# Attention and clustering block: group norms and cluster counts rearranged, filler work dealt out anew

## The chip, the cores and the metric

The kernel runs on one core of a Trainium2 chip, in 32-bit floating point. The metric is the device time of one execution in microseconds, as a median of several runs. A profile of one further execution gives the trace.

## The reference, cut to what matters

Four images `x` of 256 channels and 64 x 64 pixels go through two layers. Layer 0 is full self-attention over the 4096 pixels. Layer 1 is a clustering block, an MLP and a pointwise product:

```python
x = gamma * (v @ softmax(q^T k)^T) + x                      # layer 0
xn = group_norm(x)                                          # over all channels and pixels of an image
feat, val = conv1x1(xn, f_w), conv1x1(xn, v_w)              # 4 heads of 24 channels
# each image and head in 2 x 2 folds of 32 x 32 pixels; in each, 4 centres m (means of 16 x 16 cells)
sim = sigmoid(beta + alpha * cosine(centres, points))       # [m, n]
mask = one_hot(argmax over m); sim = sim * mask
agg = (sum_n sim[m, n] * val[n] + val_centre[m]) / (mask.sum(-1) + 1.0)
out[n] = sum_m sim[m, n] * agg[m]
y = x + ls1 * conv1x1(out, proj_w)
y = y + ls2 * mlp(group_norm(y))                            # 256 -> 1024 -> gelu -> 256
z = relu(bn(conv1x1(relu(bn(y * dw_w)), pw_w)))
```

The group norm has one group: a mean and a variance over the whole image. `mask.sum(-1)` counts the points that a centre has won.

## The kernel before

The images are worked on one after the other. For each there is an attention stage, a clustering stage (`cluster`) and an MLP stage (`mlp`). The order of every engine's instructions is the order in which the program writes them (`manual_schedule`); nothing is reordered by a planner.

**Fillers.** Where the clustering stage has short dependent steps, TensorE gets independent work to do. It is a list of small jobs, `todo`, and `fill(n)` takes the next n of them. In images 0 to 2 the list holds the projections of the next image's attention, 35 jobs: 32 halves of `v` (L316; after each second one ACT copies a finished pair out of PSUM, L324), two halves of `k` (L293, `kp`) and one of `q` (L335, `qp`). In image 3 there is no next image. There the list holds the MLP of the last 512 pixels of image 2 (`late_block`, L1073 `hlp`, L1090 `mol`, L1116 `pwl`). `fill(N)` empties the list.

**Group norm.** `group_norm` is called as `gn1` at the head of the clustering stage, and as `gn2` at the head of the MLP. The per-partition statistics are merged by L245 into `mv`. Two products with one column each (L247, L248, `gnm`) give a partition's distance from the mean, and the mean. A filler follows. On VectorE L251 copies both to `dv`, L252 adds the squared distance to the variance, L255 negates the mean. A third product (L257, `gnv`) averages the variance; `rsqrt` is L173 (add eps, VectorE), L174 (square root, ACT), a callback `meanwhile`, and L176 (reciprocal, VectorE). L265 and L266 make the factors `ga` and `gb`. In `gn1` the callback is `pooling`: it first sums the last block of pixels into its cells (`rest`, L523), then makes the pooled means (L703, L704), which L723 normalizes and `pcen` (L728) projects. In `gn2` a small ACT instruction makes ACT load the Gelu table after the last filler of the group norm (`table`, L239).

**Clustering.** The normalized image goes through the `fv` products (L866) in eight blocks. For each, VectorE writes values and raw similarities (L875, L882), and `heads` squares and sums lengths (L846 on POOL, or on VectorE for the last block; L847). `similar(f)` scales one half of the similarities and applies a tanh, `affine(f)` (L821) turns that into the sigmoid, `largest(f)` (L826 to L832) makes the one-hot mask `oh`, `weights(f)` (L836) multiplies both into `sim`. `affine(0)` is done within the loop over blocks, at the eighth. `summed` (L896) is 32 small products that add to `agg`: once with the pooling matrix, once with `sim`. The counts are 8 products of a matrix of ones with slices of `oh` (L922, `cnt`). Then L931 to L933 make the divisors `rc`, `sim` is transposed (L940), the sums are copied (L930) and transposed (`aggt`, L949), L953 makes the centres' values and `gp` (L961) projects them. The `op` products (L983) bring them back to the pixels; VectorE adds them (L995) and takes the statistics for `gn2` (L976), ACT and POOL do the other half (L1007, L1008).

**MLP.** Four POOL additions prepare weight combinations (L1171, L1172, L1173, L1176). The first block of the image is normalized (L1190) and combined (L1253 to L1256, on VectorE); then `first(nb, j)` makes a quarter of the hidden layer with seven products (`hp`, `hq`, `hr`, L1373).

Each 32-bit product appears in the trace as two records; 8 `cnt` products in four images are 64 records.

Of the kernel before, what the change touches and what calls it, by code (L numbers as in the profile page):

```python
# [9 lines left out]
AF = mybir.ActivationFunctionType  # L10
ALU = mybir.AluOpType
AX = mybir.AxisListType
# [33 lines left out]
def attention_then_cluster_block(  # L46
# [190 lines left out]
    def table(f):  # L237

        nc.scalar.activation(probe, probe, f)  # L239

    def group_norm(b, which, stats, fill, meanwhile=lambda: None):

        nm = f"{which}_{b}"
        mv = small.tile([P, 2], F32, tag="mv", name=f"mv_{nm}")
        nc.vector.bn_aggr(mv, stats.rearrange("p i s -> p (i s)"))  # L245
        ps1 = ps_a.tile([P, NB], F32, tag="a0", name=f"gnm_{nm}")
        nc.tensor.matmul(ps1[:, 0:1], left, mv[:, 0:1], start=True, stop=True)  # L247
        nc.tensor.matmul(ps1[:, 1:2], avg, mv[:, 0:1], start=True, stop=True)  # L248
        fill(1 if which == "gn1" else 2)
        dv = small.tile([P, 2], F32, tag="dv", name=f"dv_{nm}")  # L250
        nc.vector.tensor_copy(dv, ps1[:, 0:2])  # L251
        nc.vector.scalar_tensor_tensor(  # L252
            mv[:, 1:2], dv[:, 0:1], dv[:, 0:1], mv[:, 1:2], ALU.mult, ALU.add
        )
        nc.vector.tensor_scalar(dv[:, 1:2], dv[:, 1:2], -1.0, None, ALU.mult)  # L255
        ps2 = ps_a.tile([P, NB], F32, tag="a1", name=f"gnv_{nm}")
        nc.tensor.matmul(ps2[:, 0:1], avg, mv[:, 1:2], start=True, stop=True)  # L257
        rstd = small.tile([P, 1], F32, tag="rstd", name=f"rstd_{nm}")
        rsqrt(rstd, ps2[:, 0:1], GN_EPS, meanwhile)
        fill(3 if which == "gn1" else 1)  # L260
        if which == "gn2":
            table(AF.Gelu_apprx_tanh)
        ga = small.tile([P, KC], F32, tag="ga", name=f"ga_{nm}")
        gb = small.tile([P, KC], F32, tag="gb", name=f"gb_{nm}")
        nc.vector.tensor_scalar(ga, par(f"{which}_w"), rstd, None, ALU.mult)  # L265
        nc.vector.scalar_tensor_tensor(gb, ga, dv[:, 1:2], par(f"{which}_b"), ALU.mult, ALU.add)  # L266
        return ga, gb
# [428 lines left out]
    def cluster(b, ys, stats, cells, rest, fill, gelu, nxt, maxima):  # L696
# [1 line left out]
        pool = small.tile([P, KC, 4, 4], F32, tag="pool", bufs=1, name=f"pool_{b}")  # L698

        def pooling():  # L700
            rest()
            rows = cells.rearrange("p k (r two) a -> p k r two a", two=2)
            nc.vector.tensor_tensor(pool, rows[:, :, :, 0], rows[:, :, :, 1], ALU.add)  # L703
            nc.vector.tensor_scalar(pool, pool, 1.0 / 256, None, ALU.mult)  # L704

        ga, gb = group_norm(b, "gn1", stats, fill, pooling)
        xns, mix = {}, own_w["mix"]

        def norm(nb):
# [100 lines left out]
        def similar(f):  # L810

            sg = sgs[f]
            rsqrt(prns[f], prns[f], L2_EPS, lambda: table(AF.Gelu_apprx_tanh))
            nc.vector.tensor_tensor(quad(sg), quad(sg), over_m(prns[f]), ALU.mult)
            nc.scalar.activation(sg, sg, AF.Tanh, scale=ab[:, 0:1], bias=ab[:, 1:2])
            if f == 0:
                gelu(0)
                table(AF.Sqrt)

        def affine(f):  # L820
            nc.vector.tensor_scalar(sgs[f], sgs[f], 0.5, 0.5, ALU.mult, ALU.add)  # L821

        def largest(f):

            sg, o, best = sgs[f], oh[:, f * 256 : (f + 1) * 256], bests[f]
            nc.vector.tensor_reduce(best, quad(sg), AX.X, ALU.max)  # L826
            nc.vector.tensor_tensor(quad(o), quad(sg), over_m(best), ALU.is_equal)
            nc.vector.tensor_tensor(
                quad(o), quad(o), rank.unsqueeze(1).to_broadcast([P, 64, 4]), ALU.mult
            )  # L830
            nc.vector.tensor_reduce(best, quad(o), AX.X, ALU.max)
            nc.vector.tensor_tensor(quad(o), quad(o), over_m(best), ALU.is_equal)  # L832

        def weights(f):
            s = sim[:, :, 2 * f : 2 * f + 2, :16].rearrange("p j q s -> p q j s")
            nc.vector.tensor_tensor(  # L836
                s, folded(sgs[f]), folded(oh[:, f * 256 : (f + 1) * 256]), ALU.mult
            )

        later = {6: lambda: similar(0), 7: lambda: affine(0)}  # L840

        def heads(nb):

# [49 lines left out]
        def summed(w, first):  # L893
            for j in range(8):
                for q in range(4):
                    nc.tensor.matmul(  # L896
                        agg_p[q * 32 : (q + 1) * 32, :ED],
                        w(j, q),
                        vf[2 * (q // 2) + j // 4][:, (j // 2) % 2, 2 * (q % 2) + j % 2, ED:],
                        start=(first and j == 0),  # L900
                        stop=(not first and j == 7),
                    )

        fill(2)
        summed(lambda j, q: pool_w[:, j], True)
        heads(NBLK - 1)
        similar(1)
        fill(2)
        gelu(1)
        fill(3)  # L910
        table(AF.Sqrt)

        largest(0)
        affine(1)
        largest(1)
        weights(0)
        weights(1)

        cnt_p = ps_a.tile([P, NB], F32, tag="a1", name=f"cnt_{b}")
        ohs = oh.rearrange("p (q j s) -> p q j s", q=4, j=8)  # L920
        for j in range(8):
            nc.tensor.matmul(  # L922
                cnt_p[:ED, :64].rearrange("p (q s) -> p q s", q=4),
                ones[:, :ED],
                ohs[:, :, j],
                start=(j == 0),
                stop=(j == 7),
            )
        summed(lambda j, q: sim[:, j, q, :], False)
        nc.scalar.copy(sums, agg_p[:, :ED])  # L930
        nc.vector.tensor_scalar(rc[:ED], cnt_p[:ED, :64], 1.0, None, ALU.add)  # L931
        nc.vector.reciprocal(rc[:ED], rc[:ED])
# [225 lines left out]
    def mlp(b, ys, stats2, fill, nxt, blocks, turned, maxima):  # L1158
# [15 lines left out]
        few = swap.tile([P, h_n + 3, P], F32, tag="mix", name=f"w2_3_{b}")  # L1174
        w3_s, (pw_bcd, pw_bac, pw_abcd) = few[:, :h_n], (few[:, h_n + i] for i in range(3))
        nc.gpsimd.tensor_tensor(w3_s, s2_s, a12_s, ALU.add)  # L1176
        ga, gb = group_norm(b, "gn2", stats2, fill)
        fill(N)
        ob = out[b].rearrange("(k p) h w -> p k (h w)", p=P)
        pairs = {}  # L1180

# [286 lines left out]
        for nb in range(blocks):  # L1468
            end = nb == blocks - 1
            for j in range(4):  # L1470
                if j > 1:
                    rest()
                pw = (lambda: last(nb - 1, True, nc.gpsimd)) if end and j == 2 else lambda: None
                hs = first(nb, j, todo, slots, pw)
                if j > 1:
                    rest()
                if j == 0:
                    if nb:
                        rectify = finish(nb - 1, acc)
                    acc = [  # L1480
                        ps_a.tile([P, NB], F32, tag=f"a{c}", name=f"mo{c}_{b}_{nb}")
                        for c in range(KC)
                    ]
                    if not end:
                        acc += [
                            ps_m.tile([P, NB], F32, tag="m", name=f"mo{c}_{b}_{nb}")
                            for c in range(2, 4)
                        ]
                    elif nxt:

                        nc.sync.dma_start(
                            out=a21_s, in_=w2.rearrange("(k p) m -> p k m", p=P)[:, :h_n, P:]
                        )
                        nxt.q_block(1, nc.sync)
                elif j == 1:
                    assert not drips and not hooks
                    if nb:
                        rectify()
                    if not end:
                        ahead = norm(nb + 1, nc.gpsimd)  # L1500
                        if nb:
                            own = factors(nc.gpsimd, pairs[nb - 1][:, 1], pairs[nb - 1][:, 0])
                        else:
                            own = left_factors()
                elif j == 2 and nb and not end:
                    pointwise(nb - 1)
                scored = nxt and (nb, j) in at
                if scored:
                    copies = []
                    nxt.score(at[nb, j], copies, maxima)  # L1510
                    copies.pop()()
                if len(acc) == KC:
                    todo = second(nb, acc, hs, j)
                    slots = (2, 1, 1, 0) if scored else (0, 1, 1, 2)
                else:
                    todo = second_by_seven(nb, acc, hs, j, own, ahead)
                    slots = (0, 2, 2, 3)
                    if scored:
                        slots = (3, 1, 2, 1)
                    elif j == 2 and nb:  # L1520
                        slots = (3, 1, 0, 3)
# [131 lines left out]
```

## Time and profile before

| what | value |
|---|---|
| median of 3 runs | 3354.04 us (3353.42 to 3360.92) |
| the profiled execution | 3351.63 us, of which the trace spans 3349.9 us |
| TensorE busy (PE) | 3302.7 us, 99% |
| VectorE busy (DVE) | 2225.7 us, 66% |
| GpSimd busy (POOL) | 1930.9 us, 58% |
| ScalarE busy (ACT) | 1683.3 us, 50% |
| mean granted clock of TensorE | 0.998 |

Starts of the clustering stage's marks in the trace, in us:

| | image 0 | image 1 | image 2 | image 3 |
|---|---|---|---|---|
| first `gnm` | 580.63 | 1410.59 | 2241.71 | 3048.42 |
| first `fv` | 589.27 | 1419.24 | 2250.36 | 3056.95 |
| `gp` | 625.40 | 1455.37 | 2286.49 | 3092.95 |
| second `gnm` | 643.57 | 1473.54 | 2304.66 | 3111.21 |
| first `hp` | 648.66 | 1480.31 | 2309.75 | 3118.18 |
| second `hp` | 653.11 | 1484.40 | 2314.20 | 3125.18 |

In the profile PE is TensorE's products, PEld its weight loads, DVE VectorE, POOL GpSimd. A group's line gives the program line, the engine, the operation, the tiles and shapes, the count, the busy time and mean duration, and the idle time before it with what ended it. The granted clock is the share of full speed at which TensorE was allowed to run.

### The profile page before, as it was taken

Reading aid. Unit: us, or ns where it says so; the run is one execution under the profiler, and the core shown is the slowest. Engines: PE = TensorE matmul, PEld = TensorE weight load, DVE = VectorE, ACT = ScalarE, POOL = GpSimd, SP = SyncE. Lnnn points to the kernel's source line nnn. Section 1 sums busy time; section 2 is a strip of 40 time slices with the busy share of each in tenths; the row PEclk is TensorE's granted clock in tenths of the full one; section 3 lists DMA queues with packets and bytes.
Section 4 is the critical chain, followed back from the end, with each engine's and each line's share of the span. In section 5 each row is a group of like instructions: output and inputs, shape, how many; then the busy total and the mean of one; then the engine's idle time right before and its main releaser. Section 6 shows DMA issues by size and latency. Waiting matters only on the chain.

```text
span 3349.9 us, 34778 instructions
## 1 busy us (share of the span) xinstructions
PE 3302.7 (99%) x12322; PEld 1807.3 (54%) x12322; DVE 2225.7 (66%) x3546; ACT 1683.3 (50%) x2253; POOL 1930.9 (58%) x1366
## 2 busy tenths in 40 slices
PE   8999999999999999999999999999999999999999
PEld 4334444788533444578844344457873344346686
DVE  5667764677666766467766676647766766765775
ACT  5545553545555554355455555435555555544444
POOL 2655666366365676646635566554644676673664
PEclk9999999999999999999999999999999999999999
DMA  2000002000000000200000000020000000010000
GB/s 72 13 13 10 15 8 87 4 13 20 27 12 13 13 13 21 73 4 20 19 24 13 10 13 13 22 71 4 20 26 13 13 13 13 10 40 1 13 20 26
DMA packets 43102, 70.99 MB, mean 21 GB/s; under 512 B 9680, under 2 KB 18480, under 8 KB 42928
## 3 DMA queue, kind: packets, MB, share of 16 engines
q1 hardware_dynamic: 37040, 60.83, 5.5%
q10 hardware_dynamic: 5632, 7.41, 0.9%
q8 instruction: 97, 1.59, 0.2%
q14 instruction: 77, 0.63, 0.1%
q0 software_dynamic: 256, 0.52, 0.1%
HBM read 43.46 MB, written 16.89 MB: 18 GB/s over the span
## 4 chain that ended last, share of the span: by engine, by line
PE 94%; DVE 4%; POOL 1%; ACT 1%; issue 0%; DMA 0%; ACTq 0%; POOLq 0%; DVEq 0%
PE av L479 54%; PE mo L1290 9%; PE sc L365 8%; PE hq L1373 5%; PE hp L1373 3%; PE hr L1373 3%; PE fv L866 3%; PE vp L316 2%; PE mo L1274 1%; DVE st L976 1%; PE hq_pw L1373 1%; PE pw L1229 1%; PE hr_pw L1373 1%; PE hp_pw L1373 1%; DVE x L995 0%; PE qp L335 0%
## 5 line engine op out<-in xcount | busy, mean ns | idle before, releaser
L479 PE MATMUL av<-s,v 128*128 128x512 f32 x4096 | 1819.2, 598 | 0.6 <-ACT s L469 0.6
L474 POOL TENSOR_TENSOR acc<-acc,s 128x1024 f32<-128x1024 f32 x448 | 1057.7, 2361 | 538.2 <-ACT s L469 519.4
L479 PEld LDWEIGHTS av<-s,v 128*128 128x128 f32 x4096 | 759.1, 190 | 1044.7 <-issue 1034.5
L469 ACT ACTIVATE s<-s 128x1024 f32<-128x1024 f32 x512 | 540.1, 1057 | 593.0 <-DVE s L466 551.6
L466 DVE TENSOR_TENSOR s<-s,mb 128x1024 f32<-128x1024 f32 x512 | 595.8, 1206 | 19.0 <-ACT mb L450 16.4
L387 DVE TENSOR_TENSOR top<-sc,top 128x1024 f32<-128x1024 f32 x196 | 239.4, 1221 | 374.7 <-PE sc L365 374.5
L1328 ACT ACTIVATE hs<-hs,pv_s 128x256 f32<-128x256 f32 x496 | 232.5, 502 | 341.7 <-DVE hs L1364 341.7
L1290 PE MATMUL mo<-hs,w 128*128 128x256 f32 x1512 | 387.0, 382 | 0.0
L383 ACT COPY s<-sc 128x1024 f32<-128x1024 f32 x224 | 224.9, 1004 | 225.4 <-PE sc L365 225.4
L1290 PEld LDWEIGHTS mo<-hs,w 128*128 128x128 f32 x1512 | 282.5, 190 | 57.7 <-ACT hs L1328 19.8
L365 PE MATMUL sc<-q,k 32*128 32x512 f32 x2048 | 299.9, 640 | 0.4 <-ACT s L388 0.4
L390 DVE TENSOR_TENSOR top<-sc,top 128x1024 f32<-128x1024 f32 x196 | 240.1, 1225 | 72.5 <-ACT s L383 59.4
L388 ACT COPY s<-sc 128x1024 f32<-128x1024 f32 x224 | 227.1, 1014 | 66.4 <-DVE top L385 36.1
L1364 DVE TENSOR_TENSOR hs<-hq,hs 128x256 f32<-128x256 f32 x496 | 198.5, 421 | 79.7 <-PE hq L1373 69.7
L471 POOL TENSOR_TENSOR acc<-s 128x1024 f32<-128x1024 f32 x32 | 75.3, 2354 | 286.2 <-ACT s L469 286.2
L1297 POOL TENSOR_TENSOR hs<-hs 128x256 f32<-128x256 f32 x108 | 82.3, 762 | 190.9 <-ACT hs L1381 85.0
L365 PEld LDWEIGHTS sc<-q,k 32*128 32x128 f32 x2048 | 86.4, 182 | 183.1 <-issue 122.0
L1364 DVE TENSOR_TENSOR hs<-hp,hs 128x256 f32<-128x256 f32 x124 | 52.1, 420 | 134.5 <-ACT hs L1381 134.5
L1373 PE MATMUL hr<-xn,w 128*128 128x256 f32 x496 | 127.5, 379 | 0.5 <-DVE hs L1364 0.5
L316 PE MATMUL vp<-wv_s,x 128*128 128x256 f32 x512 | 125.8, 392 | 0.2 <-ACT v L324 0.2
L316 PEld LDWEIGHTS vp<-wv_s,x 128*128 128x128 f32 x512 | 94.2, 192 | 30.5 <-issue 12.0
L1373 PEld LDWEIGHTS hr<-xn,w 128*128 128x128 f32 x496 | 94.1, 190 | 19.1 <-issue 4.8
(261 smaller groups left out, 3501.0 us busy)
## 6 DMA issues: line engine op xcount, KB each, us to landing
out<-xn SPq DMA_DIRECT2D x62, 256.0 KB, 2.1
x<-in_x SPq DMA_DIRECT2D x30, 512.0 KB, 6.4
w<-in_w SPq DMA_DIRECT2D x8, 1024.0 KB, 11.0
mr<-row_mx SPq DMA_DIRECT2D x28, 256.0 KB, 3.1
rden<-row_rd SPq DMA_DIRECT2D x28, 256.0 KB, 3.2
q<-q ACTq DMA_DIRECT2D x96, 64.0 KB, 2.0
mix<-in_wfv SPq DMA_DIRECT2D x8, 192.0 KB, 8.5
q<-q SPq DMA_DIRECT2D x24, 64.0 KB, 2.0
```

The costliest lines, as they stand in the source:

```text
L316: nc.tensor.matmul(vps[0][:, i % 2, :], xs[i * P // XT][:, k, o : o + P], wv_s[:, k, :], start=(k == 0), stop=(k == KC - 1),)
L365: nc.tensor.matmul(halves[r // 2][:, r % 2, :], k_s[rows, g, :], q_s[rows, :], start=True, stop=True)
L387: nc.vector.tensor_tensor(top, halves[1], top, ALU.max)
L390: nc.vector.tensor_tensor(top, halves[0], top, ALU.max)
L466: nc.vector.tensor_tensor(sh, sh, mxs[nb].unsqueeze(1).to_broadcast([P, 2, NB]), ALU.subtract)
L469: nc.scalar.activation(sh, sh, AF.Exp)
L474: nc.gpsimd.tensor_tensor(acc, acc, s[:, 2 * h : 2 * h + 2], ALU.add)
L479: nc.tensor.matmul(av[c], own["v"][:, RG * g + quarter, c * P : (c + 1) * P], slots[u][:, quarter, :], start=(g == 0 and quarter == 0), st ...
L1290: return nc.tensor.matmul(bank[:, half * HB : (half + 1) * HB], a[:, j], t, start=start, stop=stop)
L1328: nc.scalar.activation(src, src, AF.Gelu_apprx_tanh, bias=pvc("b1", P, j + 4 * (i > 1)))
L1364: nc.vector.tensor_tensor(dst, ps, term, ALU.add)
L1373: nc.tensor.matmul(out, w, x, start=True, stop=True)
```

## The change

- In `group_norm`, L252 reads its first input from PSUM (`ps1`) in place of the copy `dv`.
- `group_norm` has a second callback, `between`, after L255. In `gn1` it is `rest`, which was the first step of `pooling`: the reduction L523 is now written ahead of `rsqrt`.
- In `gn2` the Gelu table is loaded in the callback `meanwhile`, directly after the square root.
- `affine(0)` moves out of the loop over blocks, to just before `largest(0)`.
- The sums with the pooling matrix come after the second `fill(2)`, in place of before it.
- The counts: two VectorE reductions, `count(0)` and `count(1)`, sum `oh` over the 8 slices, and one product with ones takes the place of eight. It stands after the sums with `sim`.
- Fillers: 4 in place of 3 before `largest(0)`; in `gn2` 1 and 2 in place of 2 and 1; what is left of the list comes after the first `first(0, 0)` of the MLP, in place of before its normalization.

```diff
-    def group_norm(b, which, stats, fill, meanwhile=lambda: None):
+    def group_norm(b, which, stats, fill, between=lambda: None, meanwhile=lambda: None):
...
-        fill(1 if which == "gn1" else 2)
+        fill(1)
         dv = small.tile([P, 2], F32, tag="dv", name=f"dv_{nm}")
         nc.vector.tensor_copy(dv, ps1[:, 0:2])
         nc.vector.scalar_tensor_tensor(
-            mv[:, 1:2], dv[:, 0:1], dv[:, 0:1], mv[:, 1:2], ALU.mult, ALU.add
+            mv[:, 1:2], ps1[:, 0:1], dv[:, 0:1], mv[:, 1:2], ALU.mult, ALU.add
         )
         nc.vector.tensor_scalar(dv[:, 1:2], dv[:, 1:2], -1.0, None, ALU.mult)
+        between()
         ps2 = ps_a.tile([P, NB], F32, tag="a1", name=f"gnv_{nm}")
         nc.tensor.matmul(ps2[:, 0:1], avg, mv[:, 1:2], start=True, stop=True)
         rstd = small.tile([P, 1], F32, tag="rstd", name=f"rstd_{nm}")
         rsqrt(rstd, ps2[:, 0:1], GN_EPS, meanwhile)
-        fill(3 if which == "gn1" else 1)
-        if which == "gn2":
-            table(AF.Gelu_apprx_tanh)
+        fill(3 if which == "gn1" else 2)
...
         def pooling():
-            rest()
...
-        ga, gb = group_norm(b, "gn1", stats, fill, pooling)
+        ga, gb = group_norm(b, "gn1", stats, fill, rest, pooling)
...
-        later = {6: lambda: similar(0), 7: lambda: affine(0)}
+        later = {6: lambda: similar(0)}
+
+        def count(f):
+
+            nc.vector.tensor_reduce(
+                bests[0].rearrange("p (q s) -> p q s", q=4)[:, 2 * f : 2 * f + 2],
+                folded(oh[:, f * 256 : (f + 1) * 256]).rearrange("p q j s -> p q s j"),
+                AX.X,
+                ALU.add,
+            )
...
         fill(2)
-        summed(lambda j, q: pool_w[:, j], True)
         heads(NBLK - 1)
         similar(1)
         fill(2)
+        summed(lambda j, q: pool_w[:, j], True)
         gelu(1)
-        fill(3)
+        fill(4)
         table(AF.Sqrt)
 
+        affine(0)
         largest(0)
         affine(1)
         largest(1)
         weights(0)
         weights(1)
+        summed(lambda j, q: sim[:, j, q, :], False)
+        count(0)
+        count(1)
 
         cnt_p = ps_a.tile([P, NB], F32, tag="a1", name=f"cnt_{b}")
-        ohs = oh.rearrange("p (q j s) -> p q j s", q=4, j=8)
-        for j in range(8):
-            nc.tensor.matmul(
-                cnt_p[:ED, :64].rearrange("p (q s) -> p q s", q=4),
-                ones[:, :ED],
-                ohs[:, :, j],
-                start=(j == 0),
-                stop=(j == 7),
-            )
-        summed(lambda j, q: sim[:, j, q, :], False)
+        nc.tensor.matmul(cnt_p[:ED, :64], ones[:, :ED], bests[0], start=True, stop=True)
         nc.scalar.copy(sums, agg_p[:, :ED])
...
-        ga, gb = group_norm(b, "gn2", stats2, fill)
-        fill(N)
+        ga, gb = group_norm(
+            b, "gn2", stats2, fill, meanwhile=lambda: table(AF.Gelu_apprx_tanh)
+        )
...
                 hs = first(nb, j, todo, slots, pw)
+                if nb == 0 and j == 0:
+                    fill(N)
```

## The prediction

> **What bounds the kernel now.** I read the page first, then who waited for whom on PE, then the timelines of PE, DVE, ACT and POOL through the clustering stage of all four images. The page says that TensorE sets the time:
>
> ```profile
> PE 3302.7 (99%) x12322; PEld 1807.3 (54%) x12322; DVE 2225.7 (66%) x3546; ACT 1683.3 (50%) x2253; POOL 1930.9 (58%) x1366
> ...
> PE 94%; DVE 4%; POOL 1%; ACT 1%; issue 0%; DMA 0%; ACTq 0%; POOLq 0%; DVEq 0%
> ```
>
> PE idles for 3349.9 - 3302.7 = 47 us in all. So only two things can gain: PE work that disappears, or idle in the stage that is edited. PE's waits there (us in total, how often, the longest):
>
> ```profile
> PE gnm_gn L247 <- DVE mv_gn L245: 6.4, 6, 1.9
> ...
> PE hp L1373 <- DVE hs L1364: 3.6, 4, 0.9
> ...
> PE cnt L922 <- DVE scr L832: 1.4, 1, 1.4
> ...
> PE gnv_gn L257 <- DVE dv_gn L255: 1.2, 3, 0.4
> ```
>
> With the rows for `gnv` behind L252 (0.7), and in image 3 for `gnm` behind ACT (2.6) and `hp` behind L1254 (2.6), the stage holds under 20 us of idle. Here is the first group norm of image 0 (timeline: start, duration, engine, line):
>
> ```profile
> 581.10 1.11 PE L316 MATMUL vp<-wv_s,x 128*128 128x256 f32 x4
> 581.28 0.16 DVE L251 COPY dv_gn<-gnm_gn 128x2 f32<-128x2 f32 x1 [0.70 <-PE gnm_gn L248]
> 581.31 1.26 POOL L1155 TENSOR_TENSOR w<-w 128x512 f32<-128x512 f32 x1
> 581.47 1.12 DVE L252 SCALAR_TENSOR_TENSOR mv_gn<-dv_gn,mv_gn 128x1 f32<-128x1 f32 x1
> 582.51 0.14 DVE L255 TENSOR_SCALAR dv_gn<-dv_gn 128x1 f32<-128x1 f32 x1
> ...
> 582.65 0.38 PE L257 MATMUL gnv_gn<-mv_gn,avg 128*128 128x1 f32 x2 [0.43 <-DVE dv_gn L255]
> ```
>
> L252 handles one element per partition and takes 1.12 us. It ends at 582.59, when POOL's L1155 ends (582.57). Each of its eight runs takes 0.90 to 1.12 us and ends with a POOL addition. L251, whose input is in PSUM, takes 0.16 in the middle of that POOL instruction. PE's filler (0.93 of PE time by the chain) is over at 582.22, so PE idles 0.43.
>
> **The change part by part.** Sums are against the profiled execution's own 3351.63 us (span 3349.9 and 1.73 around it), which lies 2.41 below the median 3354.04.
>
> *A, the first group norm.* L252 gets one input from PSUM; by L251 I take it at 0.16 to 0.2, bounds 0.16 and the old 1.12. It ends at 581.65, PE starts `gnv` at 582.22 instead of 582.65. Now `between` puts the cells' reduction (L523, 1.21) behind L255 and ahead of the square root; before it ran after L173. Queued behind it on DVE are L173, and through that ACT's root, L176, `ga`, `gb` and the pooled means that PE's `pcen` needs. If L255 goes at once: L255 to 581.8, reduction to 583.03, L173, root to 583.44 with L703 and L704 beside it, L176 at 583.54, L265, L266 and L723 by their rows (0.23 to 0.49) to 584.75. PE's three fillers end at 582.22 + 3.09 = 585.31, so `pcen` (585.81 before) starts PE-bound at 585.31: 0.50 gained. If L255 must wait for POOL as L252 did (to 582.57), all of this is 0.9 later, `pcen` starts at 585.55 and 0.26 is gained. The row nearest to the question is in the second group norm: L255 ran 645.24 to 645.38 with POOL's L1176 under way since 645.26, and all eight L255 take 0.14. I take 0.50. From `pcen` to the `fv` loop PE is busy but for 0.07, so it carries over. Image 3 (idle 0.33 and 0.11): 0.43. A = 3 x 0.50 + 0.43 = 1.93.
>
> The Trainium skill speaks against L255 (VectorE: DVE Perf Modes, What auto-detection actually checks; SBUF — State Buffer, Who interferes with whom): a one-source operation from SBUF to SBUF with equal shapes may take both ports, and is then blocked by POOL for a whole instruction. By that, A would be 4 x 0.26 = 1.04; the L255 row beside L1176 says otherwise.
>
> *B, from the `fv` loop to `gp`.* Per image, 8 `cnt` products (16 records, 1.33 by the chain) become one: 1.33 - 0.17 = 1.16 less PE work. One filler of 0.93 comes in earlier (3 becomes 4), taken from the second group norm. PE of image 0, from the end of `fv` at 612.04: two fillers 613.77, `kp` and `qp` 617.22, pooled sums 618.68, four fillers 622.40, sums with `sim` 623.86, `cnt` 624.03. DVE: `affine(0)` leaves a place where it hid (L821 611.36 to 612.08, while DVE waited for `fv` until 612.08) and costs a step of 0.32 (618.45 to 618.77) on the path; `weights` end at 621.69 + 0.32 = 622.01, before PE's 622.40. The two count reductions, 128x256 to 128x32, I price by L831 (0.42, step 0.46), not by the slower L523 pace with 1024 elements: done at 622.93, hidden by 0.93. At L523's 1.21 each they would end at 624.5 and cost 0.6 in images 0 to 2 and 1.0 in image 3, 2.9 in all. What is late next: `cnt` now comes after the sums, so L931, L932, L933 (622.82 to 623.88, 1.06) are no longer under them. They end at 625.16, `agg` (L953) at 625.4, `gp` at 625.46. ACT is late too: the table load (1.5 with its probe) stands behind the copy of the fourth filler, so the copy of the sums ends at 624.8 rather than 624.1; it is covered by the same wait. `gp` was at 625.40: loss 0.06. In image 3 PE waits for `weights` (3089.38 + 0.32 = 3089.70), then 1.46 of sums, 0.17, 1.06 and 0.25 give `gp` at 3092.8 for 3092.95: gain 0.15. B = 0.15 - 0.18 = 0. The saved PE work turns into idle and an earlier filler.
>
> Between `gp` and the second `gnm` DVE sets the pace (L995 and L976 run without a break from 628.04 to 642.89, PE idles 1.92 after that), so the earlier filler brings nothing there.
>
> *C, the second group norm.* Write T for the start of `gnm` (643.57). Before: first hidden product waits for L1254, at T + 5.81; the next `hp` at 653.11 waits 0.90. After: `gnm` 0.6, one filler, `gnv` at T + 1.53 (was T + 2.44), L173 at T + 1.82, root, L176 (0.16 even beside POOL's L1110 in image 3), L265 at T + 2.43. POOL's L1176 runs until 646.53 = T + 2.96, and L265 is blocked by such an addition:
>
> ```profile
> 3113.92 1.27 POOL L1110 TENSOR_TENSOR yl<-xl 128x512 f32<-128x512 f32 x1 [0.93 <-ACT xl L1101]
> 3113.97 0.16 DVE L176 RECIPROCAL rstd_gn<-rstd_gn 128x1 f32<-128x1 f32 x1 [0.32 <-ACT rstd_gn L174]
> 3114.17 1.04 DVE L265 TENSOR_SCALAR ga_gn<-pc_s,rstd_gn 128x2 f32<-128x2 f32 x1
> ```
>
> So L265 ends at T + 2.98, L1190 starts at T + 3.28 (was T + 3.74): gain 0.46; unblocked it would be 0.79. The table load moves directly behind the root, before ACT is wanted. The last filler, after the first hidden block, lies in the 0.90 wait and sticks out by 0.04. Image 3: its root waits for ACT's L1101 (3113.75, as before), gain 0. C = 3 x 0.46 - 4 x 0.04 = 1.22.
>
> *D, the clock.* After PE's idle in image 1 the granted clock fell (columns: window, its length, busy time of PE, PEld, DVE, ACT and POOL, clock, DMA, GB/s):
>
> ```profile
> 1472.00:1478.00 6.00, 4.46 (x17) 3.82 (x18) 3.24 (x10) 2.40 (x4) 4.42 (x4) 0.76 0.01 3
> 642.00:648.00 6.00, 4.43 (x23) 4.01 (x24) 4.04 (x12) 3.29 (x6) 4.45 (x4) 1.00 0.00 0
> ```
>
> From `gnm` to the second `hp` image 1 needs 10.86 us, images 0 and 2 need 9.54. With two fillers fewer ahead of the products, PE has over 1.2 us to spare there, so such a dip costs little: I count 1.1 of the 1.32. Bounds: 1.3, and -1.7 if a dip falls where PE has no slack.
>
> The Trainium skill (TensorE: Matmul & The Clock Gate, What's actually happening) lets the clock fall after an idle window of about 3.4 us. The trace shows it after 1.92 idle and two one-column products. By the page alone no gap here would count, and D would be 0.
>
> Sum: 1.93 + 0 + 1.22 + 1.1 = 4.25. Own time 3347.4; by the median, 3354.04 - 4.25 = 3349.8.
>
> **The rivals.**
>
> *R1, slower: POOL holds the whole second normalization.* In image 3 five DVE instructions in a row take 1.04 to 1.57 us beside POOL (L266 there 1.18, in image 0 0.22); from L265's start to L1254's end takes 7.13 us (3114.17 to 3121.30), against 2.44 (646.79 to 649.23). That is 4.69 per image, 14.1 for three, less A and D (3.0): 3365. It needs POOL's four additions (L1171 to L1176) to run beside L265 and what follows. Now they start 2.1 before T, and only the last meets L265. One POOL instruction later (1.27) L266 is held too, L1190 comes after T + 3.74 and C turns negative; the full price needs some 4.5 us. Against it: POOL's start follows the same L1008, which no edit delays.
>
> *R2, L252 stays slow.* It keeps one tensor and its scalar in SBUF, as L265 has, and L265 is held. Then `gnv` doesn't move in A; only the reduction ahead of the root helps, about 0.3, total 2.6: 3351.4. Against: L995, a bank and SBUF, takes 0.66 steadily beside POOL's L1008.
>
> *R3, faster by over 0.3%.* The clock's dips all go (each 1.7), and L265 is free: 4.25 + 1.0 + 3 = 8.3, 3345.7; it needs luck of the clock to reach 10.
>
> **How the numbers follow.** 0.3% is 10 us, about what a measurement can tell. The forecast 0.72 with R2 at 0.12 lie within: same 0.84. R3 with the clock beyond what I priced: faster 0.10. R1 and unknown waits: slower 0.06. The range takes the slow bounds (A down 0.9, counts up 2.9, clock up 2.8: 3356.4) and the fast ones (8.3: 3345.7), with some 2 us on either side, as the median itself lies 2.4 from the profile: 3343 to 3358.
>
> **What would show it.** Right: L252 at 0.2 beside POOL; `gnv` behind its filler without idle; two count reductions of 0.4; 4 `cnt` products in place of 32; about 0.3 idle before `gp`; `gnm` still waiting 1.9 for `mv`; idle before the first `hp`, none before the second. Wrong: L255 at about 0.9, reductions above 0.9, L266 or L1190 held by POOL in images 0 to 2, or a difference outside these stages.

## The result, and the profile after

The changed kernel takes 3349.27 us (median of 18 runs, 3347.64 to 3350.54) against 3352.55 us for the kernel before on the same chip (18 runs, 3350.52 to 3360.92). The ratio is 0.9985, with a 95% interval of 0.9978 to 0.9993. The forecast was 3349.8 us: the time, the range and the case (within 0.3%) were right. The terms of the sum were not, as the traces show.

The profiled execution of the changed kernel took 3348.09 us, with a span of 3346.3 us (before 3351.63 and 3349.9). Its line numbers are shifted a little: L257 is now L258, L265 L264, L316 L315, L523 L522, L723 and L728 L721 and L726, L832 and L836 L830 and L834, L896 L904, L922 L932, L931 to L933 L934 to L936, L953 L956, L961 L964, L1116 L1119, L1155 L1158, L1176 L1179, L1190 L1194, L1254 L1258, L1373 L1377. The new reductions are L842. In the experiments a line can lie some lines further on. The page's busy times and its shares of the chain:

```profile
PE 3301.5 (99%) x12266; PEld 1805.9 (54%) x12266; DVE 2222.5 (66%) x3554; ACT 1681.7 (50%) x2253; POOL 1931.9 (58%) x1366
...
PE 94%; DVE 4%; ACT 1%; POOL 1%; DMA 0%; issue 0%; ACTq 0%; DVEq 0%; POOLq 0%
```

PE has 56 records fewer, the `cnt` products that went, but only 1.2 us less busy time where 4 x 1.16 = 4.6 us of products went. Most of the rest came back as products at half speed: PE was busy for 19.3 us at half clock in this trace, for 9.8 in the one before (see the clock below). What PE waited for, in us in total, times, and the longest:

```profile
PE gnm_gn L247 <- DVE mv_gn L245: 4.9, 6, 1.4
...
PE hp L1377 <- DVE xn L1258: 3.3, 2, 2.6
...
PE gp L964 <- DVE scr L956: 1.4, 4, 0.5
...
PE hp L1377 <- ACT probe L239: 0.4, 1, 0.4
```

The row for `cnt` behind L832 is gone, and so are those for `gnv`. A row for `gp` behind L956 is new. Between the marks of a stage the two traces read, in us:

| stretch | before | after | gained, four images |
|---|---|---|---|
| first `gnm` to `gnv` | 2.01 (image 3: 1.90) | 1.41 | |
| `gnv` to `pcen` | 3.17 | 2.81 | |
| `pcen` to first `fv` | 3.47 (image 0: 3.45) | 3.41 | |
| A: first `gnm` to first `fv` | 8.65 (image 3: 8.53) | 7.63 | 3.94 |
| B: first `fv` to `gp` | 36.13 (image 3: 36.00) | 36.42 (image 3: 36.23) | -1.10 |
| `gp` to second `gnm` | 18.17 (image 3: 18.26) | the same | 0 |
| C and D: second `gnm` to second `hp` | 9.54, 10.87, 9.54, 13.97 | 9.19, 9.14, 9.07, 15.36 | 1.16 |

These make 4.0 us. The first `gnm` itself starts 0.74 us later (581.37 for 580.63), because the first `kp` waited 6.8 us for its weights' DMA instead of 6.0. Some 0.3 us come from the stretches in between, and 4.0 - 0.74 + 0.3 is the 3.55 us by which the span is shorter. The times of single runs differ by more than most terms, so the experiments are read by these distances, which repeat to some hundredths of a microsecond wherever the clock holds.

### The profile page after: what moved, and what is told of

Its sections match the earlier page's. It is cut to its first block, busy times and chain, and to the rows that moved or that the text cites. A ratio compares the mean times of both kernels' runs of the same rounds, so it can differ in the third digit from the quotient of the medians.

```text
span 3346.3 us, 34677 instructions
## 1 busy us (share of the span) xinstructions
PE 3301.5 (99%) x12266; PEld 1805.9 (54%) x12266; DVE 2222.5 (66%) x3554; ACT 1681.7 (50%) x2253; POOL 1931.9 (58%) x1366
## 4 chain that ended last, share of the span: by engine, by line
PE 94%; DVE 4%; ACT 1%; POOL 1%; DMA 0%; issue 0%; ACTq 0%; DVEq 0%; POOLq 0%
PE av L478 54%; PE mo L1294 9%; PE sc L364 8%; PE hq L1377 5%; PE hp L1377 3%; PE hr L1377 3%; PE fv L874 3%; PE vp L315 2%; PE mo L1278 1%; PE hq_pw L1377 1%; DVE st L979 1%; PE pw L1233 1%; PE hr_pw L1377 1%; PE hp_pw L1377 1%; DVE x L998 0%; DVE top L377 0%
## 5 line engine op out<-in xcount | busy, mean ns | idle before, releaser
L315 PE MATMUL vp<-wv_s,x 128*128 128x256 f32 x512 | 127.8, 395 | 1.9 <-ACT v L323 1.5
L1377 PE MATMUL hr<-xn,w 128*128 128x256 f32 x496 | 127.5, 379 | 0.5 <-DVE hs L1368 0.5
L315 PEld LDWEIGHTS vp<-wv_s,x 128*128 128x128 f32 x512 | 95.1, 194 | 30.2 <-issue 12.7
L1377 PEld LDWEIGHTS hr<-xn,w 128*128 128x128 f32 x496 | 94.1, 190 | 19.1 <-issue 4.8
```

Source lines behind the costliest of these rows:

```text
L315: nc.tensor.matmul(vps[0][:, i % 2, :], xs[i * P // XT][:, k, o : o + P], wv_s[:, k, :], start=(k == 0), stop=(k == KC - 1),)
L1377: nc.tensor.matmul(out, w, x, start=True, stop=True)
```

## Experiments

Each kernel is the changed one with the edit shown, unless it says otherwise. Lines starting with - are the changed kernel's.

**The first group norm, taken apart.** The first experiment gives L252 its old input back and keeps the reduction where the change put it. The second is the kernel before with L252's new input alone.

```diff
 e1_sbuf_input
-            mv[:, 1:2], ps1[:, 0:1], dv[:, 0:1], mv[:, 1:2], ALU.mult, ALU.add
+            mv[:, 1:2], dv[:, 0:1], dv[:, 0:1], mv[:, 1:2], ALU.mult, ALU.add
 e2_psum_alone (against the kernel before)
-            mv[:, 1:2], dv[:, 0:1], dv[:, 0:1], mv[:, 1:2], ALU.mult, ALU.add
+            mv[:, 1:2], ps1[:, 0:1], dv[:, 0:1], mv[:, 1:2], ALU.mult, ALU.add
```

> The changed kernel with one edit undone: L252 reads its first input from the copy dv in SBUF again. In the trace of the changed kernel the first group norm takes 7.63 us from gnm to the first fv product (8.65 before). Theory P (the PSUM input brings all of this, since the reduction and everything behind it hang on L252): L252 takes about 1.1 us again and ends with POOL's addition, gnv starts 2.0 after gnm, the reduction at 2.1, pcen at 5.1 to 5.2, fv at 8.5 to 8.6. Rival R (the reduction's earlier place brings a part of its own): fv at 8.2 to 8.4. In the second group norm of images 0 to 2, where a filler less stands in front of gnv, gnv starts at 1.8 rather than 1.41, and fv to gp stays at 36.42.

> The kernel before with one edit of the change alone: L252 reads its first input from PSUM. Theory P': L252 takes 0.22, gnv starts 1.41 after gnm (2.01 before), but the reduction still stands between the square root and the reciprocal, so pcen waits for VectorE until about 4.45 (before 5.18, changed kernel 4.22), and fv starts at 7.9: 0.75 of the 1.01 comes from the input, 0.25 from the reduction's place. If the listed idle of 0.43 were all that a wait costs, gnv would start at 1.58 and fv at 8.2. The second group norm keeps its 9.54 from gnm to the second hp in images 0 to 2 (10.9 where the clock falls), since there gnv waits for fillers and not for L252.

First `gnm` to first `fv` takes 8.34 us in e1 and 7.94 in e2, against 8.65 and 7.63. So the input alone is worth 0.71 per image, the reduction's place alone 0.31, and they add up to the 1.02 of the whole. Of e1's two readings the rival's held: the reduction's place brings a part of its own. This is image 2 of the changed kernel (timeline: start, duration, engine, line, and in brackets the idle time before):

```profile
2239.25 1.11 PE L315 MATMUL vp<-wv_s,x 128*128 128x256 f32 x4
2239.42 0.16 DVE L251 COPY dv_gn<-gnm_gn 128x2 f32<-128x2 f32 x1 [0.70 <-PE gnm_gn L248]
2239.46 1.27 POOL L1158 TENSOR_TENSOR w<-w 128x512 f32<-128x512 f32 x1
2239.62 0.22 DVE L252 SCALAR_TENSOR_TENSOR mv_gn<-gnm_gn,dv_gn,mv_gn 128x1 f32<-128x1 f32 x1
2239.75 0.14 DVE L255 TENSOR_SCALAR dv_gn<-dv_gn 128x1 f32<-128x1 f32 x1
2239.81 1.21 DVE L522 TENSOR_REDUCE cells<-x 128x8 f32<-128x1024 f32 x1
...
2240.19 0.28 PE L258 MATMUL gnv_gn<-mv_gn,avg 128*128 128x1 f32 x2
...
2243.01 0.43 PE L726 MATMUL pcen<-pool,mix 128*96 128x16 f32 x4
```

L252 takes 0.22 in the middle of POOL's addition, and L255 0.14. In e1, with both tensor inputs in SBUF, L252 is slow again, PE waits, and the reduction is late with it:

```profile
2241.93 1.12 DVE L252 SCALAR_TENSOR_TENSOR mv_gn<-dv_gn,mv_gn 128x1 f32<-128x1 f32 x1
...
2243.04 1.20 DVE L522 TENSOR_REDUCE cells<-x 128x8 f32<-128x1024 f32 x1
...
2243.11 0.38 PE L258 MATMUL gnv_gn<-mv_gn,avg 128*128 128x1 f32 x2 [0.44 <-DVE mv_gn L252]
```

In e2 `gnv` goes as early as in the changed kernel, but the reduction ends later and holds the pooled means:

```profile
2245.52 0.28 PE L257 MATMUL gnv_gn<-mv_gn,avg 128*128 128x1 f32 x2
...
2245.91 1.21 DVE L523 TENSOR_REDUCE cells<-x 128x8 f32<-128x1024 f32 x1
...
2248.19 0.49 DVE L723 TENSOR_SCALAR pool<-pool,ga_gn,gb_gn 128x16 f32<-128x16 f32 x2
...
2248.58 0.49 PE L728 MATMUL pcen<-pool,mix 128*96 128x16 f32 x4
```

Here `pcen` starts 3.06 after `gnv`, against 2.81, so PE waited 0.25 for it. The row of `pcen` has no bracket. Of such a short wait the listed idle shows a part, as at `gnv`, or nothing, as here.

**The counts.** The old eight products come back in their old place, with one filler fewer ahead of `largest(0)`. `affine(0)` stays where the change put it.

```diff
 e3_counts_old
-        fill(4)
+        fill(3)                      # and one filler more after the statistics
...
-        summed(lambda j, q: sim[:, j, q, :], False)
-        count(0)
-        count(1)
-        nc.tensor.matmul(cnt_p[:ED, :64], ones[:, :ED], bests[0], start=True, stop=True)
+        for j in range(8):
+            nc.tensor.matmul(..., ones[:, :ED], ohs[:, :, j], ...)
+        summed(lambda j, q: sim[:, j, q, :], False)
```

> The changed kernel with the counts as before (eight products ahead of the sums with sim, no reductions) and three fillers ahead of them; the fourth goes to the last fill before the second group norm. Theory C (the late single product puts the divisors L934 to L936 on the path; the PE work saved is worth nothing as VectorE sets the pace from gp to the second gnm): fv to gp falls from 36.42 to about 36.07 in images 0 to 2, and in image 3 it is 36.3 (36.23 with the change, 36.00 before), since affine(0) stays on the path there; gp to the second gnm stays at 18.17. Rival W (PE's work counts): eight products of 0.083 per record cost 1.16 more, so fv to gp or the stretch after it is longer than with the change by over 0.5.

First `fv` to `gp` took 36.33 in all four images. In image 3 that is what was expected. In the others it is not: 36.07 was expected, because I let the eight products start at once after their filler. The trace shows that they too now stand behind VectorE, whose L830 ends later with `affine(0)` on its path: in image 0 it ends at 620.87, and the first of the eight starts at 620.93, ahead of its filler's listed end (620.98). So of the 0.29 that B lost per image, 0.20 remains with the old counts. The new counts and the filler that went in for them cost 0.09 together, and gain 0.10 in image 3 (36.23). The new form of the counts in image 0 of the changed kernel:

```profile
621.67 1.07 DVE L842 TENSOR_REDUCE scr<-scr 128x32 f32<-128x256 f32 x2
621.98 1.53 PE L904 MATMUL agg<-vf,sim 128*32 128x96 f32 x64
...
623.44 0.38 PE L932 MATMUL cnt<-scr,ones 128*96 128x64 f32 x2
...
623.86 0.22 DVE L934 TENSOR_SCALAR scr<-cnt 96x64 f32<-96x64 f32 x1 [1.11 <-PE cnt L932]
...
624.70 0.22 DVE L936 TENSOR_TENSOR scr<-scr,h 96x64 f32<-96x64 f32 x1
...
625.05 0.22 DVE L956 TENSOR_TENSOR scr<-aggt,scr 96x64 f32<-96x64 f32 x1
...
625.42 0.67 PE L964 MATMUL gp<-wproj_s,scr 97*128 97x256 f32 x2 [0.30 <-DVE scr L956]
```

Both reductions (1.07 together) end 0.70 before the product that needs them. What they feed is no longer covered: from the start of `cnt` to `gp` there are 1.98 us of VectorE steps and handovers, and PE idles 0.30 at its end.

**`affine(0)` back in its place, and the counts earlier.** The next two follow from that. The first puts `affine(0)` back into the loop over blocks, where VectorE waits for `fv` anyway. The second (e7) has this edit and the next experiment's, and also counts after six of the eight slices of the sums, so that the divisors are worked out under the last two.

```diff
 e5_affine_in_loop
-        later = {6: lambda: similar(0)}
+        later = {6: lambda: similar(0), 7: lambda: affine(0)}
...
-        fill(4)
+        fill(3)                      # and one filler more after the statistics
...
-        affine(0)
 e7_tuned (e5 and e6, and)
-        summed(lambda j, q: sim[:, j, q, :], False)
+        summed(lambda j, q: sim[:, j, q, :], False, range(6))
         count(0)
         count(1)
         nc.tensor.matmul(cnt_p[:ED, :64], ones[:, :ED], bests[0], start=True, stop=True)
+        summed(lambda j, q: sim[:, j, q, :], False, range(6, 8))
```

> The changed kernel with affine(0) back in the loop over blocks (where VectorE waits for fv anyway) and three fillers instead of four ahead of the sums with sim; the fourth goes to the last fill before the second group norm. Theory C2 (from the end of fv to gp VectorE's chain to weights sets the pace, and affine(0) costs 0.32 on it; the filler is free only if PE ends it before weights): weights end 0.32 earlier, the sums start with them, and fv to gp falls from 36.42 (36.23 in image 3) to 35.9 in all four images. Rival W2 (PE's work sets the pace in images 0 to 2, the place of affine(0) nothing): 36.42 - 0.93 = 35.5 in images 0 to 2, and 36.23 stays in image 3.

> Both edits of the two kernels with affine(0) in the loop and with image 3's fillers as before, and the single count product placed after three quarters of the sums with sim. Theory Q (the divisors L934 to L936, 1.06 us behind the count product, end last ahead of gp; the two reductions end about 1.1 after weights, three quarters of the sums about as late): the wait ahead of gp goes and fv to gp falls to 35.5 to 35.7 in all images. Rival: the sums' copy and transposition end last, 35.9 as without it. Total against the changed kernel: 0.7 to 0.8 in images 0 to 2, 0.6 and 1.4 in image 3, 4 us in all.

The stretch took 35.90 in e5 (35.91 in image 3) and 35.60 in all images of e7: both as expected, 0.52 and 0.82 less than in the changed kernel in images 0 to 2, 0.32 and 0.63 in image 3. The 1.4 us that e7 was to bring in image 3's second group norm did not come (15.66 us there, see the clock). The counts of e7, image 2:

```profile
2277.80 0.38 PE L931 MATMUL cnt<-scr,ones 128*96 128x64 f32 x2
...
2278.22 0.22 DVE L934 TENSOR_SCALAR scr<-cnt 96x64 f32<-96x64 f32 x1 [0.60 <-PE cnt L931]
...
2279.05 0.22 DVE L936 TENSOR_TENSOR scr<-scr,h 96x64 f32<-96x64 f32 x1
...
2279.80 0.46 PE L964 MATMUL gp<-wproj_s,scr 97*128 97x256 f32 x1
```

The divisors' chain is the same, 0.42 after `cnt` and 1.05 long, but PE has the last sums and the transposes of `sim` beside it. In e5 the weights L834 end 32.42 after the first `fv` in image 0, where the changed kernel has 32.75, and with one filler fewer ahead of them the sums follow at once; they start at 32.24 for 32.98 and wait for L834 on the way (1.76 us for 1.53). The kernel before also has three fillers there and `affine(0)` in the loop, but the eight products: against its 36.13 the new counts of e5, with the pooling sums moved, gain 0.23 of the 1.16 us of PE work that they save. Counting earlier brings 0.30 more.

**The second group norm.** Its fillers and its table load as they were before.

```diff
 e4_gn2_old
-        fill(1)
+        fill(1 if which == "gn1" else 2)
...
-        fill(3 if which == "gn1" else 2)
+        fill(3 if which == "gn1" else 1)
+        if which == "gn2":
+            table(AF.Gelu_apprx_tanh)
...
-            b, "gn2", stats2, fill, meanwhile=lambda: table(AF.Gelu_apprx_tanh)
+            b, "gn2", stats2, fill
         )
+        fill(N)
...
-                if nb == 0 and j == 0:
-                    fill(N)
```

> The changed kernel with the second group norm dealt out as before: fillers 2 and 1, the Gelu table after them, the rest of the list ahead of the first normalization. Theory G (gnv and with it the whole normalization come a filler earlier, and the last filler hides in the wait before the second hp): gnm to the second hp is 9.54 again in images 0 to 2 where the clock is full (9.07 with the change in image 2) and 10.9 where it falls (9.14 with the change in image 1). In image 3, where the change took 15.36 for 13.97 before, it is 14.0 to 14.4 as PE does one more product ahead of the long wait. Rival N (the new input of L252 brings the gain here too): 9.1 to 9.3 in images with a full clock.

Second `gnm` to second `hp` took 9.72 in images 0 to 2, not the 9.54 of the kernel before, and 14.51 in image 3 for an expected 14.0 to 14.4. The 0.18 between them is a side effect. One filler more had been dealt out earlier in the stage, so the pairs of `v` are complete one filler sooner, and a copy of `v` now stands on ACT ahead of the square root (image 2 of e4, ACT):

```profile
2304.16 0.58 ACT L325 COPY v<-vp 128x512 f32<-128x512 f32 x1 [1.94 <-PE vp L317]
2304.64 0.21 ACT L174 ACTIVATE rstd_gn<-rstd_gn 128x1 f32<-128x1 f32 x1
```

So the new deal in `gn2` is worth 0.47 against the kernel before and 0.65 against the old deal in its new place. In the changed kernel, image 2, the path runs like this:

```profile
2302.69 1.27 POOL L1179 TENSOR_TENSOR w<-w,w 128x512 f32<-128x512 f32 x1
...
2303.16 0.16 DVE L176 RECIPROCAL rstd_gn<-rstd_gn 128x1 f32<-128x1 f32 x1 [0.27 <-ACT rstd_gn L174]
2303.36 0.62 DVE L264 TENSOR_SCALAR ga_gn<-pc_s,rstd_gn 128x2 f32<-128x2 f32 x1
2304.02 0.22 DVE L265 SCALAR_TENSOR_TENSOR gb_gn<-ga_gn,dv_gn,pc_s 128x2 f32<-128x2 f32 x1
...
2304.92 0.67 PE L1377 MATMUL hp<-xn,w 128*128 128x256 f32 x2 [0.39 <-ACT probe L239]
```

L264 begins at `gnm` + 2.35 and ends with POOL's L1179 at + 2.97. What follows is not held. `hp` is put down to ACT's probe, which ended at 2304.64; its operand came from VectorE's L1194 (2304.28 to 2304.83 in the same timeline), 0.09 before it starts. To test that POOL's last addition costs what I think, the eighth kernel moves it to where POOL has nothing to do, ahead of the `op` products. It is e7 with:

```diff
 e8_pool_early (against e7; e10_pool_early is the same kernel, timed)
         fill(1)
+        early()                      # w3_s = s2_s + a12_s, on POOL
         stats2 = small.tile([P, 2 * NBLK, 6], F32, tag="stats", name=f"st2_{b}")
...
-        nc.gpsimd.tensor_tensor(w3_s, s2_s, a12_s, ALU.add)
```

> The tuned kernel, with the fourth of POOL's additions of weights done ahead of the op products, where POOL is idle. With the change L264 (the factor ga) is held by that addition until 2.97 after gnm (0.62 for 0.23). Theory H (POOL holds VectorE there): L264 takes 0.23, the normalization and the second hp come 0.39 earlier, gnm to the second hp 8.6 to 8.8 in images 0 to 2 (9.07 to 9.19), and in image 3 one VectorE instruction less is held, 12.9 to 13.4. Rival: the table load, 1.5 behind the root, then ends last (hp waits for ACT), and nothing or under 0.1 is gained.

```profile
2299.29 0.17 DVE L176 RECIPROCAL rstd_gn<-rstd_gn 128x1 f32<-128x1 f32 x1 [0.27 <-ACT rstd_gn L174]
2299.49 0.23 DVE L264 TENSOR_SCALAR ga_gn<-pc_s,rstd_gn 128x2 f32<-128x2 f32 x1
```

In this timeline of e8, image 2, L264 takes 0.23, and second `gnm` to second `hp` takes 8.68 in images 0 to 2 against 9.08, and 13.02 in image 3: as expected.

**The clock and the place of the last fillers.** Here stands the one loss that I had not foreseen, 1.39 us in image 3. PE around its first hidden block, in the changed kernel:

```profile
3109.22 3.57 PE L1119 MATMUL pwl<-xl,wpw_s 128*128 128x512 f32 x4
3113.22 0.67 PE L1377 MATMUL hp<-xn,w 128*128 128x256 f32 x2 [0.44 <-DVE xn L1194]
3116.49 1.19 PE L1377 MATMUL hp<-xn,w_abcd 128*128 128x256 f32 x2 [2.59 <-DVE xn L1258]
3117.47 1.06 PE L1377 MATMUL hq<-xn,w 128*128 128x256 f32 x2
```

An `hp` product takes 0.67 ahead of the long wait for L1258 and 1.19 behind it. The sixth experiment puts what is left of the list ahead of the first normalization again, in image 3 alone:

```diff
 e6_last_fill
             b, "gn2", stats2, fill, meanwhile=lambda: table(AF.Gelu_apprx_tanh)
         )
+        if not nxt:
+            fill(N)
```

> The changed kernel, but in image 3 alone what is left of the filler list is done ahead of the first normalization, as before. Theory D (image 3 has lost 1.4 us from gnm to the second hp, 15.36 for 13.97, because PE has one product less in the long wait for VectorE and the granted clock falls for more windows of 3.41 us): 13.9 to 14.6 with at most two such windows there. Rival L (it was chance, by where the windows lie): 15.3 or more again. Images 0 to 2 as with the change: 9.1 to 9.2.

Image 3 took 13.99, as in the kernel before. The granted clock in the same stretch, second `gnm` to second `hp` of image 3, and in image 0 (windows view: window, length, busy time of PE, PEld, DVE, ACT, POOL, granted clock, DMA, GB/s), first the kernel before:

```profile
643.00:656.00 13.00, 11.41 (x53) 9.43 (x54) 8.14 (x22) 6.41 (x13) 4.63 (x5) 1.00 0.00 0
...
3111.21:3125.18 13.97, 9.71 (x28) 5.19 (x29) 11.38 (x19) 5.24 (x10) 7.82 (x6) 0.88 0.10 38
```

The changed kernel:

```profile
643.00:653.00 10.00, 9.37 (x37) 7.66 (x38) 6.67 (x21) 4.53 (x9) 3.55 (x3) 0.83 0.00 0
...
3106.24:3121.60 15.36, 12.29 (x28) 6.95 (x29) 9.79 (x19) 4.62 (x9) 7.83 (x6) 0.69 0.05 18
```

And e6, image 3, and e2, image 0, which has the old deal of fillers and two falls of the clock:

```profile
3105.96:3119.95 13.99, 10.49 (x29) 5.98 (x29) 9.80 (x19) 5.41 (x10) 7.83 (x6) 0.80 0.10 39
```

```profile
643.00:656.00 13.00, 11.80 (x41) 9.80 (x42) 6.37 (x21) 4.82 (x10) 3.28 (x3) 0.74 0.00 0
```

The clock falls to a half for stretches of 3.41 us: one of them in 10 us gives 1 - 0.5 x 0.341 = 0.83, and two in 13 us give 0.74, as the rows have. Whether it falls differs between executions of one kernel: in image 0 it fell in the changed kernel's first trace and not in e9, which is the same kernel. What a fall costs depends on the deal of fillers. In images 0 to 2 with the old deal it cost 1.33 (10.87 for 9.54, before), 1.69 (11.23, e2) and 2.94 (12.48, two stretches, e2). With the new deal it cost 0.05 to 0.6 (9.13 to 9.65 for 9.08, in the changed kernel, e6 and e9). In image 3 all five traces with the last fillers behind the first hidden block took 15.36 to 16.72 (the changed kernel twice, e1, e3, e5). Of those with them ahead four took 13.97 to 14.51 (before, e2, e4, e6), and one (e7) 15.66 with three stretches at half clock; e8 and e10, which have POOL's addition early as well, took 13.02 and 13.05. So the place of the fillers decides most of it, and the chance of the phase some of it.

The windows show how. In each of the twelve traces all stretches begin on one grid of 3.41 us. From 30 us on, 51 falls begin within the traces, and in the window of the grid just ahead of each fall PE's listed idle was 1.44 us or more. Of the windows at full clock, none of the 11513 with less idle was followed by a fall, 16 of 39 with 1.44 to 2.0 us were, and all 35 with more. e1 and e6 met image 3 in nearly the same phase (their first falls begin 1.19 and 1.24 us ahead of `gnm`). In e1, with the last filler behind the first hidden block, one window has 0.71 us of idle ahead of the first `hp` and 1.4 of the long wait, and the clock falls:

```profile
3117.12:3120.53 3.41, 1.29 (x4) 0.30 (x2) 3.38 (x3) 0.21 (x1) 3.41 (x3) 1.00 0.21 77
3120.53:3123.94 3.41, 2.23 (x5) 1.83 (x6) 2.19 (x5) 0.37 (x1) 0.29 (x1) 0.50 0.00 0
```

In e6 the filler (1.02) lies in that window, the idle of the wait is shared by two windows, and it does not fall:

```profile
3111.55:3114.96 3.41, 2.07 (x6) 0.68 (x4) 3.38 (x3) 1.04 (x2) 3.41 (x3) 1.00 0.26 99
3114.96:3118.37 3.41, 2.15 (x10) 1.95 (x11) 2.41 (x6) 0.37 (x1) 0.37 (x1) 1.00 0.16 59
```

The listed wait for VectorE's L1258 is 2.60 in both, as it was before the change.

**Timed.** The changed kernel again and e10, in five rounds on one chip with the kernel before:

> The changed kernel as it is, timed beside the kernel before and the tuned one on the same chip. By the stages of its profile (4.0 us gained from the first gnm to the second hp of the four images) and the spread of its runs: 0.9985 of before, 0.9975 to 0.9995; a rerun of the stages gives 7.63, 36.42 and 18.17 again, and 15.3 to 16.7 in image 3 if the falls of the clock there belong to it.

> The tuned kernel with POOL's fourth addition early, timed. By its profile's stages (first gnm to second hp: 69.98 us in images 0 to 2 for 71.2 to 71.4 with the change, and 74.5 for 77.5 in image 3) 6 to 7 us below the changed kernel: 0.9965 of before, 0.9955 to 0.9975. If the stages' gains were eaten by the clock, 0.998 or more.

| kernel | median, us | lowest to highest | runs | ratio to before, 95% |
|---|---|---|---|---|
| before | 3353.46 | 3350.99 to 3360.97 | 15 | |
| e9, the change | 3349.70 | 3346.74 to 3351.28 | 11 | 0.9985 (0.9976 to 0.9994) |
| e10 | 3340.96 | 3340.44 to 3341.18 | 5 | 0.9958 (0.9944 to 0.9972) |

The single executions of the others gave 3354.32 (e1), 3352.77 (e2), 3348.67 (e3) and 3348.52 (e4) with the kernel before at 3354.15 beside them, and 3347.54 (e5), 3346.41 (e6), 3346.01 (e7) and 3341.70 (e8) with it at 3354.60.

e10 beats both kernels. Its ratio lies in the expected range; the 8.7 us by which its median lies below e9's are more than the expected 6 to 7. In the traces e10's span is 8.7 us shorter than e9's (3339.4 and 3348.1): 3.1 from `fv` to `gp` (0.82 in images 0 to 2, 0.63 in image 3), 2.1 in the second group norms of images 0 to 2 (8.67 and twice 8.68 for 9.08, 9.65 and 9.42, of which 0.9 are e9's falls of the clock), 2.3 in image 3 (13.05 for 15.38), and 1.3 between images 2 and 3, where e9 took 729.16 us from the third `hp` to the next `gnm` and the changed kernel's first trace took 727.86 like e10. e9's clock was at half for two stretches there (from 2513.6 us on), that of the other two for one. That last part is no gain of e10's.

## Why the prediction was right, and where it was not

**The time was right by luck: errors of both signs cancelled.** The prediction had A at 1.93, B at 0 and C with D at 2.32. Measured: 3.94, -1.10 and 1.16, with the later start of 0.74 and the 0.3 from between the stages. The errors add up to 2.01 - 1.10 - 1.16 - 0.74 + 0.3 = -0.7, as the profiled execution shows (3348.09 for 3347.4).

**A, mis-sized by half.** The mechanism was right in each step: L252 at 0.22, L255 not held, `gnv` behind its filler, `pcen` bound by PE. The term that failed is 0.50 per image: the 0.43 of PE's listed idle at `gnv`, and the 0.07 between the fillers' listed end and `pcen`, taken for the whole wait. At `gnv` the listed end of the filler is a model. In the kernel before the filler ran 581.10 to 582.21 as listed. In the changed kernel `gnv` starts 0.94 after the start of the same filler, 0.17 before its listed end. So PE stood for 0.60, not 0.43. A one-column product that is issued after a stop takes 0.38 rather than 0.28 (e1 and e2), and the next product starts that much later: 0.10 more. At `pcen` PE waited 0.25, and 0.06 more ahead of `fv`, where next to nothing was listed. 0.60 + 0.11 + 0.31 is the 1.02 that was measured, and e1 and e2 show the two parts.

The choice on L255 held: 0.14 beside L1158. The Trainium skill (VectorE: DVE Perf Modes, What auto-detection actually checks) asks for outermost non-unit dimensions that are even or equal. L255 with one element per partition has no such dimension, which may be why the rule doesn't reach it, and L264 with two was held (0.62). No run here changes the shape, so this reading is argued only.

**B, the wrong step is the tail from `cnt` to `gp`.** It was priced at 1.60 (0.17 for the product, 0.07 to L934, 1.06, 0.24 to and through L956, 0.06 to `gp`) and took 1.98: L934 starts 0.42 after the start of `cnt` (0.24 in the sum), L956 0.13 after L936 (0.02), `gp` 0.15 after L956 (0.06). `cnt` itself started 0.15 earlier after `fv` than forecast, so the loss is 0.06 + 0.38 - 0.15 = 0.29. In image 3 the same 0.38 turned a gain of 0.15 into a loss of 0.23. (The terms named there for image 3's tail are 1.48; the 3092.8 needs the 1.60 of the other images, with both handovers.) The reductions cost 0.53 each for 0.42, and were hidden as forecast. That 1.16 us less PE work per image is worth nothing in this form was forecast; e5 and e7 show that it begins to pay when the VectorE steps around it are taken off the path.

**C, right.** 0.42 per image forecast (0.46 and the filler that sticks out by 0.04), 0.47 measured in image 2, with L264 held until `gnm` + 2.97 for a forecast 2.98. (`gnv`, given there as T + 2.44 before, starts at T + 2.28 in the timeline; it now starts at T + 1.41.) e8 shows that POOL's addition was the holder, and 0.40 the price. R1 did not happen, since only the last of the four additions met L264, as the prediction argued. R2 is ruled out by L252's 0.22. (The 0.66 of L995 is its spacing; each of its 32 runs takes 0.73 to 0.75.)

**D, half right.** Image 1 gained 1.73 with C in it, for 1.1 + 0.42. The missed step is image 3, put at no gain: the deal that takes the last fillers out of the way of the first products in images 0 to 2 leaves PE idle ahead of image 3's first `hp` as well (0.44, and 0.71 in e1), the clock falls once more behind the long wait, and 1.39 is lost. The bound of -1.7 for a fall without slack covers its size, but the place was not named. e6 brings the 1.39 back; e7, with the fillers in the same place, lost it again by another phase. Beyond the profile of one execution, the smaller price of a fall also goes with the narrower spread of the runs (2.9 us for 10.4 in the 18 pairs); that it causes it is argued from the traces, since the timed runs have none.

Unchanged as forecast: `gp` to second `gnm`, 18.17 in every kernel. The listed wait of `gnm` for `mv` fell from 1.9 to 1.4 there without any effect, because part of it is now listed as PE's wait for a copy of `v` (0.4). The start of the first norm, later by 0.74, lies outside the edited stages. It was 581.15 and 581.25 in e9 and e10, so 580.63 was the odd one; its cause was not tried.

## What to carry to other kernels

The listed idle of a busy TensorE was here a lower bound of a short wait (0.43 for 0.60, nothing for 0.25): compare the distances between marks of two traces instead. When work is taken from the engine that the page calls the bound, follow the chain of the engine that feeds it, handovers of 0.13 to 0.42 us included; here the products saved were worth nothing until the VectorE steps around them were moved. Filler work was worth more ahead of image 3's long wait than behind it, because enough idle in one window of the clock's grid cost the clock behind it too.

## What the hardware showed that was not expected

A VectorE instruction on one element per partition took 1.12 us beside a POOL addition with both its tensors in SBUF (L252 in e1), and 0.22 with one of them in PSUM. L255, with one tensor input, took 0.14 from SBUF. Two elements in SBUF took 0.62 (held by what was left of one addition) and 0.23 without one (e8).

The granted clock fell to half after little idle: in image 0 of the changed kernel it was 0.83 over 643 to 653, after 1.44 us of listed idle ahead of `gnm` and two one-column products. In e6 a window with the same listed idle (640.30 to 643.71) was not followed by a fall, so 1.44 lies at the edge; from 2.0 us on it always fell here. The Trainium skill (TensorE: Matmul & The Clock Gate, What's actually happening) has half the clock in free-running windows of about 3.4 us, which these rows agree with, but an idle window as the condition, which they do not show: the listed idle is under half of one.
